# A bias row asked for by another queue, and five pieces of dense work set between score splits, in a two-layer graph and expert kernel

## The chip, the cores and the metric

The kernel runs on one core of a Trainium2 chip. The core has five engines that work side by side, each on its own list of instructions: TensorE (PE in the profile, with its weight loads as PEld), VectorE (DVE), ScalarE (ACT), GpSimd (POOL) and SyncE (SP). SP, ACT and POOL also ask for transfers (DMAs), which 16 DMA engines carry out. The metric is the device time in microseconds (us) of one execution. Before the change the median of 7 runs is 1937.58 us (1932.46 to 1940.60).

## The reference

Two layers work on x, 128 graphs of 64 nodes with 256 features, so 8192 nodes. Each layer has a graph part and a feed-forward part; shortened:

```python
# layer 0, graph part: softplus(xn @ W_self + (I - A_norm) xn @ W_neigh), added to x
# layer 0, feed-forward: every node goes to the one of 8 experts with the highest chance
H = gelu(layernorm(x) @ W1 + b1)                      # 256 -> 1024
probs = softmax(H @ Wg + bg)
assign = argmax(probs)
for e in range(8):
    y = H @ Wd[e] + bd[e]                             # 1024 -> 256; bd[e] is one row of 256
    out = out + where(assign == e, probs[:, e:e+1] * y, 0.0)
x = x + out
# layer 1, graph part: attention inside each graph, layer norm, gelu, added to x
# layer 1, feed-forward: a graph attention over 1048576 edges (and self loops) gives each
# node a score for each of 4 experts
h = (layernorm(x) @ W_gat).reshape(M, HEADS, NUM_EXPERTS)
a_src, a_dst = (h * att_src).sum(-1), (h * att_dst).sum(-1)
e = leaky_relu(a_src[src] + a_dst[dst], 0.2)          # one value an edge and head
alpha = softmax of e over the edges that end in one node
agg = segment_sum(h[src] * alpha, dst)
scores = layernorm(agg).mean over heads
topk_s, topk_i = top_k(scores, 2); w = softmax(topk_s)
for ei in range(4):
    g = where(topk_i == ei, w, 0.0).sum(-1)
    out = out + g * (gelu(z @ W1[ei] + b1[ei]) @ W2[ei] + b2[ei])   # 256 -> 512 -> 256
x = x + out
```

## The kernel before

The nodes are held as 64 tiles of 128 rows, and four tiles (GR) make a group, so there are 16 groups. x stays in on-chip memory for the whole run. The code is a set of Python generators. Each `yield` ends a small piece of work, and the loops that call `next` mix the pieces of several generators. A scheduler then puts the instructions of each engine in an order, from what each depends on, the order in which the code traced them, and a model of their times; inside `with tc.issue_after(i)` an instruction stays behind `i` on its engine. Completion of a transfer that SP or ACT asked for is told by one of eight semaphores. They are handed out in turn, in the scheduler's order, to the transfers of both queues alike. Who takes a semaphore again first waits until the transfer that had it before has landed, whichever queue asked for that one.

**First place: the early slots of layer 0.** A slot is a tile of 128 rows that all belong to one expert. Hidden rows are sent to their expert's place in memory (`hrows`) by POOL, group by group (line 872). Eight slots (EARLY) are already full before the last two groups are through, and `early_slots` (lines 934 to 997) works on them while the last group is finished. It loads two short lists into registers: the rows' places for SP (line 936), the expert numbers for ACT and PE (line 943). For slot t, `load(t)` issues two transposing loads from SP (line 957), three slots ahead (AHEAD); their targets `hT` come from ten buffers (`bh`) that the last group still uses. `bias_of(t)` asks for the expert's bias row, broadcast to 128 partitions (128 KB), into buffer z2 or z3 by turns (lines 969 and 970), from ACT. The first call, `bias_of(0)`, stands ahead of the first loads. Eight matrix products (line 987) make the slot's result, DVE adds the bias row (line 995), and ACT asks for the store of the sum (line 996). So ACT's queue holds in turn: bias 0, bias 1, store 0, bias 2, store 1, bias 3, store 2, and so on. In the same stretch DVE and PE count keys of edges (lines 209 and 348).

**Second place: the scores of the destinations.** After the branch at line 2110 (a rare path for lists that overflow), `td`, 128 x 512 values in f32, is cut into three bf16 pieces `td3`: three copies (line 2322) and two subtractions (line 2324) on DVE. The pieces are later multiplied with one-hot matrices on PE (line 1976), for 16 lists of edges (`edges_of_lists`).

**Units of dense work.** Of layer 1's 16 groups, 8 (DENSE) are put through all four experts before it is known which a node needs. `units = dense()` (lines 1518 to 1537) yields these in units: per group and expert four "h" units (two products, and a gelu on ACT, lines 1490 and 1494) and four "y" units (four products, and DVE's sum with the bias, lines 1500 and 1504). That is 8 x 4 x 8 = 256 units. They are taken as filler all through layer 1, and the trace shows each product of f32 numbers as two: an h unit is four records, a y unit is eight. The takers, in order, are: the end of layer 1's graph part (up to line 1765, filled up to a whole expert); a step after each yield of `prologue` and two `sort`s (lines 2053 to 2055); two in three of the 162 steps of `edges_of_lists` (lines 2349 and 2350); the rest of `sending` (line 2499); a loop that fills up to a whole expert:

```python
            while (n + 1) % (NH1 + GR):
                g, n = next(units)
            adds.append(add)
            for _ in range(1 * (NH1 + GR)):
                g, n = next(units)
```

Up to `adds.append`, each y is stored (line 1527) and read again later (`kept`, line 2371); from there on it is added to x at once (line 2355). What is left of the units runs at the very end, beside `back`:

```python
        steps = back(PARTS - 1)
        for n, _ in enumerate(units):
            next(steps, None)
```

**The pairs and the way back.** The other 8 groups go only to the two experts that a node needs. Their rows are sent to slots, `pairs` runs 38 pairs of slots, and `back(h)` (lines 2466 to 2487) fetches the results for half h: 32 gathers by POOL (line 2474) into seven buffers, and five steps later a copy (line 2480, through 1516) and, for each second one, two weighted sums into x (line 2485) and the store of a finished tile (line 2486). `back(h)` has 37 steps. Its copy is kept behind the last gelu or sum of the unit traced before it (`pace`, line 1515). A gather needs the buffer of the gather seven before, which the copy frees, so gathers go at the pace of the units. `back(1)` is the one that runs at the end, after the last pair.

Of the kernel before, what the change touches and what calls it, by code (L numbers as in the profile page):

```python
# [22 lines left out]
P = 128  # L23
NT = 64
N = P * NT
D = 256
# [61 lines left out]
def kernel(  # L88
# [31 lines left out]
    nc = tc.nc  # L120
# [341 lines left out]
    with tc.tile_pool(name="w0", bufs=1, reuse_waits="tile") as w0, tc.tile_pool(name="kp", bufs=1, reuse_waits="tile") as kp:  # L462
# [30 lines left out]
        with tc.tile_pool(name="bg1", bufs=1, reuse_waits="tile") as bg1, tc.tile_pool(  # L493
# [20 lines left out]
            with tc.tile_pool(name="b2", bufs=1, reuse_waits="tile") as b2, tc.tile_pool(  # L514
# [419 lines left out]
                def early_slots():  # L934

                    _, rows_at = nc.values_load_multi_w_load_instructions(
                        early_row,
                        engines=(mybir.EngineType.SP,),
                        min_val=0,
                        max_val=E0 * N - P,  # L940
                        skip_runtime_bounds_check_because=why,
                    )
                    _, ex = nc.values_load_multi_w_load_instructions(
                        early_e,
                        engines=(mybir.EngineType.Activation, mybir.EngineType.PE),
                        min_val=0,
                        max_val=E0 - 1,
                        skip_runtime_bounds_check_because=why,
                    )
                    loaded = {}  # L950

                    def load(t):

                        loaded[t] = []
                        for i in range(0, FD, GR * P):
                            h = bh.tile([P, GR * P], F32, name="hT")
                            got = nc.sync.dma_start_transpose(
                                h.bitcast(U16).rearrange("p (q r) -> p q r", q=GR),
                                hrows[bass.ds(rows_at[t] * 2, 2 * P), i : i + GR * P],
                            )  # L960
                            for other in sends[-PART * GR :]:
                                tc.declare_no_dep(got.ins, other, reason="rows of an early tile were sent before")
                            loaded[t].append(h)

                    bds_ = {}

                    def bias_of(t):

                        bds_[t] = b2.tile([P, D], F32, name=f"z{2 + t % 2}")
                        nc.scalar.dma_start(bds_[t], f0_bd[bass.ds(ex[t], 1), :].to_broadcast([P, D]))  # L970

                    bias_of(0)
                    for t in range(AHEAD):
                        load(t)
                    yield
                    for t in range(EARLY):
                        if t + AHEAD < EARLY:
                            load(t + AHEAD)
                        if t + 2 == EARLY:
                            y_last = bh.tile([P, GR * P], F32, name="hT")[:, 0:D]  # L980
                        hT = loaded.pop(t)
                        if t + 1 < EARLY:
                            bias_of(t + 1)
                        bd = bds_.pop(t)
                        py = psb.tile([P, GR * P], F32, name="ph")[:, 0:D]
                        for q in range(NH):
                            nc.tensor.matmul(
                                py,
                                hT[q // GR][:, q % GR * P : q % GR * P + P],
                                wd[:, bass.ds(ex[t], 1), q, :].rearrange("p e f -> p (e f)"),  # L990
                                start=(q == 0),
                                stop=(q == NH - 1),
                            )
                        y = y_last if t == EARLY - 1 else b2.tile([P, D], F32, name=f"z{t % 2}")
                        V.tensor_tensor(y, py, bd, ALU.add)
                        nc.scalar.dma_start(yrows[(NSLOT + t) * P : (NSLOT + t + 1) * P, :], y)
                        yield
# [232 lines left out]
                biases = {}  # L1230
                tables, bias = slot_tables(), bias_tables()
                early = early_slots()
                for t, _ in enumerate(early):
                    next(tables, None)
# [283 lines left out]
    def dense():  # L1518

        for g in range(DENSE):  # L1520

            def take(e, k, y):
                if adds:
                    adds[0](GR * g + k, e, y)
                else:
                    n_kept[g] = e + 1
                    behind[:] = [nc.sync.dma_start(ystore[g, k, :, e * D : e * D + D], y).ins]

            if g == 0:
                prepare(0, to)  # L1530
            for n, _ in enumerate(experts(g, take)):

                if n == (0 if to["two"] else NEXP * (NH1 + GR) - GR - 1) and g + 1 < DENSE and g + 1 not in zTs:
                    prepare(g + 1, to)
                yield (g, n)

    units = dense()
# [754 lines left out]
    with tc.tile_pool(name="ga", bufs=1, reuse_waits="tile") as ga, tc.tile_pool(  # L2292
        name="em", bufs=2, reuse_waits="tile"
    ) as emp, tc.tile_pool(name="psm", bufs=1, space=PSUM, reuse_waits="tile") as psm:
        before = ga.tile([P, P], BF16, name="before")
        ones = ga.tile([P, P], BF16, name="ones")


        later = ga.tile([NEXP * RT, NEXP * RT + NEXP], BF16, name="later")
        for v in (before, ones, later):  # L2300
            nc.gpsimd.memset(v, 1.0)
        of_tile = later[:, 0 : NEXP * RT].rearrange("p (e t) -> p e t", e=NEXP)
        of_all = later[:, NEXP * RT :]
        for v, pattern, row, base, op in (
            (before, [[1, P]], -1, 0, ALU.is_gt),
            (of_tile, [[RT, NEXP], [1, RT]], -1, 0, ALU.is_gt),
            (of_tile, [[-RT, NEXP], [0, RT]], 1, 0, ALU.is_ge),
            (of_all, [[-RT, NEXP]], 1, 0, ALU.is_ge),
            (of_all, [[RT, NEXP]], -1, RT, ALU.is_gt),
        ):  # L2310
            nc.gpsimd.affine_select(
                v, v, pattern=pattern, compare_op=op, fill=0.0, base=base, channel_multiplier=row
            )
        iota_s = ga.tile([P, PAIRS], F32, name="iota_s")
        nc.gpsimd.iota(
            iota_s, pattern=[[1, PAIRS]], base=0, channel_multiplier=0, allow_small_or_imprecise_dtypes=True
        )

        td3 = ga.tile([P, 3, NT * 2 * HEADS], BF16, name="td3")
        left_over = td.rearrange("p t c -> p (t c)")  # L2320
        for j in range(3):
            V.tensor_copy(td3[:, j, :], left_over)
            if j < 2:
                V.tensor_tensor(left_over, left_over, td3[:, j, :], ALU.subtract)

        def routes():

            ranks = {}
            for h in range(PARTS):
                yield from gates(ga, T0 + h * RT, T0 + h * RT + RT, ranks)  # L2330
                yield from route(h, ga, ranks, to["ph"])

        steps = routes()
        zeros = ((h, i) for h in range(PARTS) for i in range(PAIRS))
        for taken, _ in enumerate(edges_of_lists(emp, psm, td3)):

            if taken % 3 == 0:
                for h, i in zeros:
                    nc.sync.dma_start(
                        zslots[h][2 * P * i : 2 * P * i + 2 * P].rearrange("(k p) f -> p k f", p=P),  # L2340
                        none.unsqueeze(1).to_broadcast([P, 2, D]),
                    )
                    break
            if taken > ET * (ROUTED // PARTS + 2):
                next(steps, None)

            if taken >= ET * NB:
                next(sending)
            if taken % 3 != 2:
                next(units)  # L2350
        for _ in steps:
            pass
# [229 lines left out]
```

## Time and profile before

| what | value |
|---|---|
| median of 7 runs | 1937.58 us |
| the profiled execution's own time | 1938.42 us |
| its span, first to last instruction | 1936.7 us |
| granted TensorE clock, mean | 0.982 |
| PE busy | 1826.3 us, 94% |
| DVE busy | 1356.6 us, 70% |
| ACT busy | 920.5 us, 48% |
| POOL busy | 444.0 us, 23% |
| early slots' stretch | about 590 to 660 us |
| branch at line 2110, scores, lists | 1297 to about 1560 us |
| pairs | about 1595 to 1874 us |
| last units and the way back | 1874 to 1936.7 us |

The profile is of one execution. Its times count from the first instruction; the time of the run is 1.7 us more than the span. A line of groups or waits names the engine, the tile and the source line. "ACTq" and "SPq" are the queues from which those engines ask for transfers, and "PEldq" is PE's own sequencer. A time in brackets is what the engine stood idle before, with what ended the idle time by the profile's inference.

### The profile page before, as it was taken

The page shows a single profiled execution, that of the slowest core. Times are in us where ns is not written, and L with a number is a line of the kernel's source. Part 1 is how long each engine was busy: PE and PEld are TensorE (multiplying, and loading weights), DVE is VectorE, ACT ScalarE, POOL GpSimd, SP SyncE. Part 2 cuts the span into 40 slices and gives each one's busy share as a digit, 9 for nine tenths or more (in the row PEclk, how much of TensorE's full clock was granted, in tenths as well). Part 3 has the DMA queues.
Part 4 walks back from the last instruction along what each step waited for, and adds up shares of the span by engine and source line. Part 5 has one row for each costly group of instructions (what it writes and reads, how often), then busy time and mean ns, then how long its engine had stood idle before and what let it go on. Part 6 is the DMA issues. An engine that isn't in the chain of part 4 may idle for free. (4 is left out here: it accounts for less than half of the span.)

```text
span 1936.7 us, 31223 instructions
## 1 busy us (share of the span) xinstructions
PE 1826.3 (94%) x10125; PEld 1274.9 (66%) x10125; DVE 1356.6 (70%) x4472; ACT 920.5 (48%) x1612; POOL 444.0 (23%) x465
## 2 busy tenths in 40 slices
PE   7899999998999798899878999999999999999998
PEld 5455555554456687788555666656767768888885
DVE  7798898895668799967598656848888542334435
ACT  4877886886752000000677676323333433334322
POOL 3011111010111011111221000016677633303214
PEclk9999999999999899999979999989999999999999
DMA  9762323242416877698115111562222358979943
GB/s 297 204 194 86 113 71 116 86 141 97 145 74 134 176 172 154 144 180 162 50 60 167 51 55 54 195 184 60 69 53 71 103 166 259 309 241 284 283 140 120
DMA packets 365895, 276.97 MB, mean 143 GB/s; under 512 B 195464, under 2 KB 327456, under 8 KB 365728
## 3 DMA queue, kind: packets, MB, share of 16 engines
q1 hardware_dynamic: 320896, 204.41, 38.3%
q0 software_dynamic: 23040, 60.22, 9.7%
q10 hardware_dynamic: 21792, 10.27, 2.2%
q8 instruction: 86, 1.41, 0.3%
q14 instruction: 81, 0.66, 0.1%
HBM read 115.91 MB, written 123.18 MB: 123 GB/s over the span
## 5 line engine op out<-in xcount | busy, mean ns | idle before, releaser
L505 PE MATMUL ph<-zT,w 128*128 128x512 f32 x512 | 248.4, 610 | 6.1 <-ACT hT L509 6.1
L1348 PE MATMUL py<-wd,hTt 128*128 x960 | 219.5, 382 | 0.0
L1348 PEld LDWEIGHTS py<-wd,hTt 128*128 128x128 f32 x960 | 178.8, 191 | 23.4
L1963 POOL DMA_INDIRECT got<-tsrc,esrc x144 | 155.9, 1083 | 157.0 <-DVE esrc L1934 77.5
L1500 PE MATMUL py<-w,hT 128*128 128x256 f32 x736 | 172.5, 387 | 6.3 <-DVE kt L1902 4.7
L1490 PE MATMUL ph<-zT,w 128*128 128x512 f32 x368 | 169.8, 604 | 0.0
L1356 ACT COPY y<-py 128x256 f32<-128x256 f32 x60 | 22.4, 373 | 290.9 <-PE py L1348 226.5
L1500 PEld LDWEIGHTS py<-w,hT 128*128 128x128 f32 x736 | 138.2, 192 | 32.0 <-issue 8.8
L872 POOL DMA_INDIRECT hrows<-rows,pos x64 | 65.4, 1022 | 395.3 <-ACT wd L654 75.0
L2444 ACT ACTIVATE hT<-ph,b1e 128x256 f32<-128x256 f32 x152 | 72.1, 474 | 172.3 <-PE ph L2440 95.3
L505 PEld LDWEIGHTS ph<-zT,w 128*128 128x128 f32 x512 | 90.6, 193 | 83.5 <-issue 73.1
L1494 ACT ACTIVATE hT<-ph,b 128x512 f32<-128x512 f32 x92 | 63.1, 688 | 165.9 <-PE ph L1490 164.3
L2440 PE MATMUL ph<-zTp,w1e 128*128 128x256 f32 x608 | 137.5, 379 | 0.7 <-ACT zTp L2422 0.7
L2453 PE MATMUL py<-w,hT 128*128 x608 | 137.5, 379 | 0.0
L2461 DVE TENSOR_TENSOR y<-py,b2e 128x256 f32<-128x256 f32 x76 | 32.3, 424 | 149.3 <-PE py L2453 144.7
L668 PE MATMUL pre<-wd 128*128 128x512 f32 x256 | 126.3, 606 | 2.1 <-ACT wd L654 1.3
L509 ACT ACTIVATE hT<-ph,b 128x512 f32<-128x512 f32 x128 | 87.9, 689 | 81.0 <-PE ph L505 77.1
L2440 PEld LDWEIGHTS ph<-zTp,w1e 128*128 128x128 f32 x608 | 115.4, 190 | 16.6 <-ACT zTp L2422 0.9
L808 ACT COPY rows<-tz 128x1024 uint16<-128x1024 uint16 x112 | 110.3, 1020 | 25.8 <-DMA hrows<-rows,pos 13.9
L2453 PEld LDWEIGHTS py<-w,hT 128*128 128x128 f32 x608 | 112.6, 190 | 13.8
L1490 PEld LDWEIGHTS ph<-zT,w 128*128 128x128 f32 x368 | 67.8, 191 | 68.0 <-issue 67.1
L807 PEld LDWEIGHTS tz<-ident,hT 128*128 128x128 f32 x512 | 60.6, 142 | 72.6 <-ACT rows L808 34.3
(505 smaller groups left out, 3748.6 us busy)
## 6 DMA issues: line engine op xcount, KB each, us to landing
w1e<-in_L_ffn_W_dram SPq DMA_DIRECT2D x38, 512.0 KB
yin<-ystore SPq DMA_DIRECT2D x24, 512.0 KB
yrows<-none SPq DMA_DIRECT2D x10, 1024.0 KB
zslots<-none SPq DMA_DIRECT2D x38, 256.0 KB
zin<-zslots SPq DMA_DIRECT2D x38, 256.0 KB
yslots<-y SPq DMA_DIRECT2D x76, 128.0 KB
ystore<-y SPq DMA_DIRECT2D x72, 128.0 KB
x<-in_x_dram SPq DMA_DIRECT2D x8, 1024.0 KB
```

The source lines that it names most:

```text
L505: nc.tensor.matmul(ph, w1[:, c, q * P : q * P + P], zT[:, c, :], start=(c == 0), stop=(c == 1))
L509: gelus.append(S.activation(hT, ph, AF.Gelu, bias=b1[:, q : q + 1]).ins)
L668: nc.tensor.matmul(pre, xnT[:, c, n * P : n * P + P], wcat[:, c, :], start=(c == 0), stop=(c == 1),)
L808: copy(rows[:, :, :, q * P : q * P + P], th.bitcast(U16).rearrange("p (k n h) -> p k h n", k=GR, h=2),)
L872: nc.gpsimd.indirect_dma_start(hrows.rearrange("(r h) f -> r (h f)", h=2), bass.IndirectOffsetOnAxis(ap=pos[:, t : t + 1], axis=0), rows[: ...
L1348: nc.tensor.matmul(py, hT[:, q, :], wd[:, bass.ds(e, 1), q, :].rearrange("p e f -> p (e f)"), start=False, stop=(q == NH - 1),)
L1490: nc.tensor.matmul(ph, w1[:, e, c, q * P : q * P + P], zT[:, c, :], start=(c == 0), stop=(c == 1))
L1500: nc.tensor.matmul(py, hTs[q][:, k * P : k * P + P], w2[:, e, q, :], start=(q == 0), stop=(q == NH1 - 1))
L1963: nc.gpsimd.indirect_dma_start(got, None, tsrc, bass.IndirectOffsetOnAxis(ap=esrc[:, b, at : at + 1], axis=0))
L2440: nc.tensor.matmul(ph, w1e[:, c, q * P : q * P + P], zT[:, c, :], start=(c == 0), stop=(c == 1))
L2444: pace[:] = [S, S.activation(hT, ph, AF.Gelu, bias=b1e[:, q : q + 1]).ins]
L2453: nc.tensor.matmul(py, hTs[q][:, k * P : k * P + P], w2[:, e, q, :].rearrange("p e f -> p (e f)"), start=(q == 0), stop=(q == NH1 - 1),)
```

## The change

There are two edits. In `early_slots`, the expert numbers are loaded into registers of SP too, and the first early slot's bias row (t = 0) is asked for by SP, where it stands ahead of the transposing loads; all later bias rows stay on ACT. In the split of the scores, one unit of dense work is taken from `units` after each copy and after each subtraction, five units in all; nothing is taken out elsewhere.

```diff
                     _, ex = nc.values_load_multi_w_load_instructions(
                         early_e,
-                        engines=(mybir.EngineType.Activation, mybir.EngineType.PE),
+                        engines=(mybir.EngineType.SP, mybir.EngineType.Activation, mybir.EngineType.PE),
                         min_val=0,
                         max_val=E0 - 1,
...
                         bds_[t] = b2.tile([P, D], F32, name=f"z{2 + t % 2}")
-                        nc.scalar.dma_start(bds_[t], f0_bd[bass.ds(ex[t], 1), :].to_broadcast([P, D]))
+                        queue = nc.scalar if t else nc.sync
+                        queue.dma_start(bds_[t], f0_bd[bass.ds(ex[t], 1), :].to_broadcast([P, D]))
...
         for j in range(3):
             V.tensor_copy(td3[:, j, :], left_over)
+            next(units)
             if j < 2:
                 V.tensor_tensor(left_over, left_over, td3[:, j, :], ALU.subtract)
+                next(units)
```

## The prediction

> **What bounds the kernel now.** I read the page first, then the busy times by stretches, then the waits and the timelines at the two places of the change, and last the timeline of the end.
>
> ```profile
> PE 1826.3 (94%) x10125; PEld 1274.9 (66%) x10125; DVE 1356.6 (70%) x4472; ACT 920.5 (48%) x1612; POOL 444.0 (23%) x465
> ```
>
> PE bounds the run as a whole; by stretches (length, then busy time of PE, PEld, DVE, ACT and POOL, the granted clock, the DMA engines' share and GB/s):
>
> ```profile
> 590.00:660.00 70.00, 55.39 (x463) 41.76 (x461) 51.49 (x199) 10.88 (x13) 6.68 (x7) 0.93 0.81 162
> 1256.00:1302.00 46.00, 40.13 (x166) 23.71 (x167) 23.50 (x74) 14.35 (x18) 6.75 (x14) 0.94 0.72 199
> 1302.00:1560.00 258.00, 257.24 (x1759) 182.44 (x1759) 199.17 (x751) 97.43 (x192) 172.46 (x161) 0.99 0.28 75
> ...
> 1596.00:1874.00 278.00, 278.00 (x1363) 244.86 (x1362) 99.24 (x233) 103.84 (x235) 64.20 (x64) 1.00 0.82 260
> 1874.00:1937.00 63.00, 55.21 (x193) 36.24 (x191) 31.77 (x85) 14.51 (x28) 32.16 (x32) 0.98 0.36 111
> ```
>
> From 1302 to 1874 us PE is without a break (257.24 of 258, 278.00 of 278). Whatever is moved about inside that stretch gains nothing. Only the stretches around it have room: 14.6 us idle in the first, 5.9 in the second, 7.8 in the last. The waits of 590 to 680 us show the largest single stall (total, times, longest):
>
> ```profile
> PE pre L348 <- DVE key L209: 13.4, 5, 10.2
> DVE z L995 <- DMA z<-in_L_ffn_bd_dram: 10.7, 1, 10.7
> ```
>
> DVE stands 10.7 us at a slot's sum with its bias row, the key counts behind it on DVE stand too, and PE stands 10.2 us for them. Which row is late, ACT's queue tells (start, duration):
>
> ```profile
> 604.84 0.93 ACTq L970 DMA_DIRECT2D z<-in_L_ffn_bd_dram  x2
> ...
> 614.78 0.34 ACTq L970 DMA_DIRECT2D z<-in_L_ffn_bd_dram  x1
> 625.17 0.35 ACTq L996 DMA_DIRECT2D yrows<-z  x1
> 634.34 0.34 ACTq L970 DMA_DIRECT2D z<-in_L_ffn_bd_dram  x1
> ```
>
> The first two requests, at 604.84, are bias 0 and 1. Bias 2 is asked for at 614.78, bias 3 only at 634.34, and DVE's wait ends at 637.87, at the fourth sum. The late row is bias 3, not bias 0: the first sum ran at 613.75 with no idle time ahead of it. By the trace's semaphore records, store 1 (625.17) waited until the ninth transposing load, issued at 614.85, had landed (625.10), and bias 3 until the tenth, issued at 616.33, had (634.32). Both only take over the semaphore of that load.
>
> At the second place, PE's first work after the branch, and the branch (min/median/max, ns):
>
> ```profile
> 1301.64 1.62 PE L1500 MATMUL py<-w,hT 128*128 128x256 f32 x3 [4.67 <-DVE kt L1902]
> ```
>
> ```profile
> L2110 PEldq COMPARE_BRANCH  x2: 64/2186/4307, 1292.3 to 1297.2; - x2
> ```
>
> The wait is booked on DVE (kt), and the chain of waits runs through the scores there. But PE's own sequencer is in the branch for 4307 ns from 1297.17, which fills 4.31 of the 4.67. No score holds PE.
>
> The end: a gather, PE's last products, the last gather, the copy after the last unit's sum, the last weighted sums.
>
> ```profile
> 1916.37 0.94 POOL L2474 DMA_INDIRECT back<-yslots,place  x1 [0.79 <-DVE yb L1516]
> ...
> 1922.14 7.07 PE L1500 MATMUL py<-w,hT 128*128 128x256 f32 x32
> ...
> 1926.69 0.94 POOL L2474 DMA_INDIRECT back<-yslots,place  x1 [0.70 <-DVE yb L1516]
> ...
> 1929.59 0.28 DVE L1516 COPY yb<-back 128x256 f32<-128x256 f32 x1
> ...
> 1932.78 0.99 DVE L2485 SCALAR_TENSOR_TENSOR x<-yb,weight,x 128x256 f32<-128x256 f32 x2
> ```
>
> PE ends at 1929.21, the run 7.5 us later, since five steps of the way back come after the last unit.
>
> **The change part by part.** *Bias 0 on SP.* SP gains one register load (ACT's took 0.76, SP's own 1.20), a request (0.39 on ACT) and 0.07 to 0.13 of address work: 1.2 to 1.8 us ahead of the first transposing load, which so starts near 597.6 instead of 596.08 and is through SP at 599.1. The second is issued at 600.43 in any case, since it waits 2.78 us for PE to free its buffer. That wait hides SP's added work; without it, up to 1.8 us would pass on to all loads. Nothing else is queued on SP; POOL's queue isn't touched. ACT loses one request of 0.4 us with nothing waiting behind.
>
> What the row itself does: the two rows of 604.84 took 59, 52, 16 and 2% of the DMA engines in the windows of 2 us from 604 to 612, 2.6 us of all sixteen, so 1.3 each. Meanwhile the fifth and sixth transposing loads took 2.71 and 2.36 us of SP against the least of 1.23. From 605 to 640 the DMA engines are at 0.88 to 1.26 of their time; from 596 to 600 at 0.29. So 1.3 us of work leaves the crowded stretch. The tenth load, and with it bias 3, may land 1.3 us earlier; then the eleventh is late next (635.58, before the fifth slot would need it). I take -1.3.
>
> Bounds: if the order of the semaphores shifts so that bias 3 takes another than the tenth load's, PE waits at 634.32 for that load itself, instead of starting the fifth slot at 639.98: -5.6, and -1.8 more if its eight products, 3.76 us after the stall against 1.97 before it, run at full clock. If the cover on SP is gone: +1.8. So -7.4 to +1.8. I stay near the small end because the turn of the semaphores stays the same: bias 0 and the loads only change places at the head of the row, and store 1 and bias 3 come as many transfers later as before.
>
> A rule that speaks against this part: the Trainium skill, "DMA: Bandwidth & Descriptors", section "Issuing engines are not separate DMA queues", has all queues end on the same 16 engines, so that another issuer saves issue time alone. By it alone this part gains at most ACT's 0.4 us, and the sum would be +7.6 instead of +6.7.
>
> *Five units among the scores.* The five DVE operations (three of 0.42, two of 0.68 us) remain. PE gets five units (a unit is 6.87/4 = 1.72 us) ahead of the lists. Nothing there waits for DVE, so the move by itself is worth 0; what hides it is PE's unbroken work to 1874. Bounds: -4.7, if units closed all of the wait; +1.5, the two waits of 0.69 and 0.86 us that PE has now at 1559 and 1562, if they came twice. I take 0, by the branch's row.
>
> But units are counted, and the fill loop rounds up. Stored results:
>
> ```profile
> L1527 SPq DMA_DIRECT2D ystore<-y x72: 319/320/667, 1278.1 to 1584.2; - x72
> L1527 SPq DMA_DIRECT2D ystore<-yin x36: 319/320/527, 1053.6 to 1256.3; - x36
> ```
>
> 108 stored y are 27 experts, 216 units. They come about as 72 (the graph part, 36 stores) + 20 (prologue 8 yields, two sorts 6 each) + 108 (two in three of 162) + 14 (32 yields of `sending` less 18) = 214, and 2 to fill the expert. With five more it is 219, and the loop takes 5 to fill 224. Then eight units with direct sums, as now. So 24 units are left for the end instead of 32: one expert, 8 x 1.72 = 13.8 us of PE, moves from behind the pairs to ahead of them. PE's sum stays, and it ends at 1929.2 as before. Four results more are stored and read again, 1.0 MB, which PE's work hides.
>
> The way back doesn't move with it. It can only start when the last pair is stored, now 13.8 us later (first gather 1877.08, then 1890.9), and 37 steps have 24 units beside them, not 32. After the last unit 13 steps remain instead of 5. Gather 25 (counting from 0) needs the buffer that the copy after the last unit frees: 1916.37 + 13.77 = 1930.14. The six after it follow at POOL's free rate, 1.25 us (1877.08, 1878.33, 1879.58): the last at 1937.64. A gather lands 2.7 to 3.3 us after its issue (least, median): 1940.3 to 1940.9. Copy and two sums take 1.2 (1932.57 to 1933.77), store and close 2.9 (1933.77 to 1936.7): 1944.4 to 1945.0, so +7.7 to +8.3. I take +8.0. DVE isn't late: 13 steps at 0.6 are done at 1938. If the copies ran ahead of the last unit, the cost would fall towards 0; `pace` keeps them behind it. If each gather took the 1.48 of the slowest free step, +9.4.
>
> Sum: -1.3 + 0 + 8.0 = +6.7. The profiled execution, 1938.42 with a span of 1936.7, would be 1945.1; it lies 0.84 above the median of the runs, so I forecast 1937.58 + 6.7 = 1944.3.
>
> **The rivals.** *The stall goes (not slower).* The added register load and request shift the loads in the scheduler's order past store 0 and bias 2; bias 3 inherits a semaphore long free and is issued with store 1 or before. Price -5.6 to -7.4, so +0.6 to +2.4 in all: 1938.2 to 1940.0. For it: in the order of the requests the loads stand close around store 0. Against: store 1 itself needed from 625.17 to 635.41 to land in the same crowd, and bias 3 would follow behind it. It decides from 4.1 us of gain on, where the whole comes under 0.2%.
>
> *The branch's wait is DVE's (not slower).* If the profile's booking is right, five units close 4.7 us: 1944.3 - 4.7 = 1939.6. The branch's 4307 ns speaks against it. A page would speak for it: the Trainium skill, "Advanced Engine Details and Errata", section "Control Flow Timing", gives a compare-and-branch about 108 ns; by it 4.2 us would be left to DVE and the sum would be +2.5; PE's row has forty times that figure.
>
> *The end isn't longer.* If the units' count comes to the same multiple of eight, or the gathers run ahead of the units, only -1.3 is left: 1936.3. Against it stand the count and the seven buffers.
>
> *SP's cover is gone.* The loads come 1.8 later and the stall with them, no gain: +9.8, 1947.4.
>
> **How the numbers follow.** 0.2% (3.9 us) is about what a measurement of this kernel can tell from no change. Forecast, slower: 0.64; cover gone, slower: 0.12; the stall goes: 0.12, of which 0.02 on to faster; DVE's wait closed: 0.04, same; end not longer: 0.08, of which 0.03 faster. Same holds 0.10 + 0.04 + 0.05 = 0.19; faster 0.05; slower 0.76. The range reaches from the case in which the stall goes (1938.2) to the lost cover (1947.4), with half a microsecond at each end for the median's own spread. The likeliest case alone has 1942 to 1946.
>
> **What would show it.** Right: the stored y's after the graph part grow from 72 to 76, 24 units after the last pair, about 8 us more between PE's last product and the end; the fourth sum's wait for its bias still near 9 us. Wrong: no wait at that sum; PE's first product after the branch without its gap; gathers that all come before PE's end.

## The result and the profile after

The changed kernel takes 1945.38 us in the median of 19 runs (1939.75 to 1950.39), the kernel before 1937.58 in 46. The ratio is 1.0042, with a 95% interval from 1.0033 to 1.0051. That is 8.1 us slower (6.4 to 9.9); the prediction had 6.7 us.

One profiled execution misleads here. That of the changed kernel took 1940.16 us, 5.2 less than its median, and its span is 1938.4 us against 1936.7 before. Read by the two spans alone, the change would cost 1.7 us. What that execution had, and a second profiled execution of the same kernel hadn't, is found below.

The page's line for PE, and the stretches of the changed kernel (length, busy time of PE, PEld, DVE, ACT and POOL, granted clock, DMA share, GB/s):

```profile
PE 1831.0 (94%) x10125; PEld 1278.0 (66%) x10125; DVE 1359.9 (70%) x4474; ACT 921.7 (48%) x1612; POOL 443.8 (23%) x465
```

```profile
590.00:660.00 70.00, 64.74 (x502) 48.14 (x501) 60.09 (x245) 12.24 (x15) 8.04 (x8) 0.93 0.82 180
1256.00:1302.00 46.00, 42.20 (x168) 26.89 (x168) 21.74 (x67) 13.66 (x17) 6.74 (x14) 0.96 0.67 180
1302.00:1560.00 258.00, 256.45 (x1762) 181.31 (x1761) 196.28 (x736) 100.53 (x195) 175.43 (x160) 1.00 0.28 73
1596.00:1874.00 278.00, 277.33 (x1360) 244.11 (x1359) 102.05 (x240) 102.62 (x233) 64.08 (x64) 1.00 0.82 261
1874.00:1938.00 64.00, 47.12 (x171) 32.11 (x169) 31.45 (x85) 12.31 (x24) 31.90 (x32) 0.90 0.38 115
```

PE still has no break worth naming from 1302 to 1874 us (256.45 of 258, 277.33 of 278). The two ends of the table have moved in opposite directions. In the early slots PE is busy for 64.74 us of 70, where it was 55.39. In the last stretch it is busy for 47.12 of 64, where it was 55.21 of 63.

The waits of 590 to 680 us, SP's first requests and its tenth transposing load, ACT's queue and POOL's first send of the last group, all of this execution:

```profile
PE pre L348 <- DVE key L209: 4.3, 5, 2.1
...
DVE z L996 <- DMA z<-in_L_ffn_bd_dram: 1.1, 1, 1.1
```

```profile
599.67 1.36 SPq L957 DMA_TRANSPOSE hT<-hrows  x1
601.89 0.39 SPq L971 DMA_DIRECT2D z<-in_L_ffn_bd_dram  x1
...
618.37 1.23 SPq L957 DMA_TRANSPOSE hT<-hrows  x1
```

```profile
608.36 0.39 ACTq L971 DMA_DIRECT2D z<-in_L_ffn_bd_dram  x1
...
619.26 0.36 ACTq L997 DMA_DIRECT2D yrows<-z  x1
619.84 0.50 ACTq L971 DMA_DIRECT2D z<-in_L_ffn_bd_dram  x1
623.18 0.35 ACTq L997 DMA_DIRECT2D yrows<-z  x1
623.75 0.37 ACTq L971 DMA_DIRECT2D z<-in_L_ffn_bd_dram  x1
```

```profile
620.07 1.14 POOL L872 DMA_INDIRECT hrows<-rows,pos  x1 [23.25 <-issue]
```

The fourth sum waited 1.1 us for its bias row instead of 10.7. Bias 0, which the source has ahead of the transposing loads, goes out behind the first of them: the scheduler has put it there, at 601.89. The lines of ACT's queue are, in order, bias 1, store 0, bias 2, store 1 and bias 3. Bias 3 went out at 623.75, 3.7 us after POOL's first send; before it went out at 634.34, 19.3 us after that send (615.01). It still takes over the semaphore of the tenth transposing load. But that load was issued at 618.37, 1.7 us ahead of the first send, and by its semaphore's records had landed at 621.69; bias 3 came right behind store 1, which stands ahead of it in ACT's queue. Before, the load was issued at 616.33, 1.3 us behind the first send, and needed until 634.32.

The branch and PE's first work after it:

```profile
L2111 PEldq COMPARE_BRANCH  x2: 64/1726/3389, 1286.3 to 1291.2; - x2
```

```profile
1294.77 2.47 PE L1501 MATMUL py<-w,hT 128*128 128x256 f32 x5 [3.75 <-DVE td L2326]
```

PE's gap of 4.67 us has become one of 3.75. The branch in it has gone from 4307 to 3389 ns, and the gap has shrunk by no more than that. The five units haven't closed it.

The stored results, and the end: PE's last products, copies and gathers of the way back, the last weighted sums; then, before and after, the closing instruction on POOL's queue (its longest record is the one at the end).

```profile
L1528 SPq DMA_DIRECT2D ystore<-y x76: 319/320/1502, 1271.9 to 1588.0; - x76
```

```profile
1914.05 7.07 PE L1501 MATMUL py<-w,hT 128*128 128x256 f32 x32
...
1921.49 0.28 DVE L1517 COPY yb<-back 128x256 f32<-128x256 f32 x1
...
1922.05 0.94 POOL L2477 DMA_INDIRECT back<-yslots,place  x1 [0.78 <-DVE yb L1517]
...
1928.59 0.95 POOL L2477 DMA_INDIRECT back<-yslots,place  x1 [0.30 <-DVE x L2488]
...
1929.84 0.95 POOL L2477 DMA_INDIRECT back<-yslots,place  x1 [0.30 <-DVE x L2488]
...
1932.68 0.29 DVE L1517 COPY yb<-back 128x256 f32<-128x256 f32 x1 [0.54 <-DMA back<-yslots,place]
1932.89 1.00 DVE L2488 SCALAR_TENSOR_TENSOR x<-yb,weight,x 128x256 f32<-128x256 f32 x2
```

```profile
L2577 POOLq DRAIN  x3: 40/112/7946, 1926.5 to 1936.4; - x3
```

```profile
L2580 POOLq DRAIN  x3: 40/113/11766, 1925.8 to 1938.1; - x3
```

76 results are stored after the graph part instead of 72, so 24 units are left behind the last pair. PE ends at 1921.12, and seven gathers are issued after that, the last at 1929.84. The last sums end at 1933.89 and the run at 1938.4, so PE's last product is 17.3 us ahead of the end, against 7.5 before. The close itself has changed hands. POOL's DRAIN ends at 1937.56, and the run 0.86 us after it; SP, which waits for the last store, was through at 1936.19. Before, the DRAIN ended at 1934.41, and SP was the last with 1935.83.

### The profile page after: what moved, and what is told of

The parts are those of the page before. It is cut to its first block, busy times and chain, and to the rows that moved or that the text cites. A ratio compares the mean times of both kernels' runs of the same rounds, so it can differ in the third digit from the quotient of the medians.

```text
span 1938.4 us, 31245 instructions
## 1 busy us (share of the span) xinstructions
PE 1831.0 (94%) x10125; PEld 1278.0 (66%) x10125; DVE 1359.9 (70%) x4474; ACT 921.7 (48%) x1612; POOL 443.8 (23%) x465
```

## The experiments

The twelve runs were made in four sets, each on one chip, and each ratio is to runs of the kernel before on the same chip. The chips differ: the kernel before took 1959.4, 1965.2 and 1958.4 us (medians) on those of the first three sets, and 1939.9 on that of the last. So only ratios are compared between sets. A difference in microseconds is the ratio times the median of before, with the interval's ends in brackets.

### First set: each edit alone, and the tail

The first edit alone:

```diff
-                        engines=(mybir.EngineType.Activation, mybir.EngineType.PE),
+                        engines=(mybir.EngineType.SP, mybir.EngineType.Activation, mybir.EngineType.PE),
...
-                        nc.scalar.dma_start(bds_[t], f0_bd[bass.ds(ex[t], 1), :].to_broadcast([P, D]))
+                        queue = nc.scalar if t else nc.sync
+                        queue.dma_start(bds_[t], f0_bd[bass.ds(ex[t], 1), :].to_broadcast([P, D]))
```

> Only the first edit: bias 0 is asked for by SyncE. Theory A (a race decides the early slots, the tail sets the rest): the wait of the fourth sum for its bias row is short where the loads get ahead of the last group's sends and about 10 us where they don't; if the tail alone costs 9.8 us, as the two profiles have it (17.3 us from PE's last product to the end against 7.5), then 8.1 - 9.8 = -1.7 us is left for this edit as a median: 1935.9 us, with PE's end to the run's end still 7.5 us. Theory B (the stall is gone for good, as the one profile of the changed kernel shows it): -9 us, 1928.6, and the second edit costs 17. Theory C (as predicted): -1.3 us, 1936.3, the fourth sum's wait still near 9 us.

Measured: 0.9982 [0.9959, 1.0004], -3.5 us (-8.0 to +0.8). PE's gap at the fourth sum was 3.1 us.

The second edit alone:

```diff
             V.tensor_copy(td3[:, j, :], left_over)
+            next(units)
             if j < 2:
                 V.tensor_tensor(left_over, left_over, td3[:, j, :], ALU.subtract)
+                next(units)
```

> Only the second edit: five units among the score splits. Theory A: +9.8 us less the 0.9 by which PE's gap after the branch was shorter, 1946.5 us, 24 units after the last pair, about 17 us from PE's last product to the end, the fourth early sum's wait near 10 us again in most executions. Theory B: +17 us, 1954.6. Theory C (as predicted): +8.0 us, 1945.6.

Measured: 1.0079 [1.0050, 1.0109], +15.5 us (9.8 to 21.4); 17.3 us from PE's last product to the end; PE's gap at the fourth sum 10.5 us.

The tail alone:

```diff
-            for _ in range(1 * (NH1 + GR)):
+            for _ in range(2 * (NH1 + GR)):
```

> The kernel before with eight units more taken by the loop after adds.append: nothing among the score splits, bias 0 on ACT, but 24 units left for the end as in the changed kernel. If the second edit costs only by the units that the end loses: the same as with the second edit alone, +8 to +10 us (1945.6 to 1947.6), about 17 us from PE's last product to the end. If it is the place among the scores that costs: within 2 us of the kernel before, 1935.6 to 1939.6.

Measured: 1.0045 [1.0016, 1.0074], +8.8 us (3.1 to 14.5); 17.3 us from PE's last product to the end. The last stores and the last gather of the way back of this kernel:

```profile
1954.10 10.78 SPq L2486 DMA_DIRECT2D out_dram<-x  x7
...
1960.42 0.95 POOL L2474 DMA_INDIRECT back<-yslots,place  x1 [0.30 <-DVE x L2485]
```

PE's last product ends at 1951.69, 8.7 us ahead of that gather. The loss of eight units at the end costs this by itself, with nothing put among the scores. The second edit cost 6.7 us more than that, with intervals that overlap, so its place came into question.

The tail the other way:

```diff
-            for _ in range(1 * (NH1 + GR)):
+            for _ in range(0 * (NH1 + GR)):
```

> The kernel before with eight units fewer taken there, so 40 are left for the end. Theory of the tail: all 37 steps of the way back have a unit beside them, PE's last product comes when it did, and the end is set by the last unit's sum and its store, 3 to 4 us after PE instead of 7.5: -3.7 us, 1933.9 us. Rival: the pairs can't start 13.8 us earlier, because their rows or weights aren't there, and PE stands before them: 0 to +13.8 us.

Measured: 1.0012 [0.9988, 1.0035], +2.4 us (-2.4 to +6.9). The end came 3.9 us after PE's last product, as the tail theory has it. PE's timeline ahead of the first pair shows that the rival came true as well:

```profile
1597.83 2.11 PE L1500 MATMUL py<-w,hT 128*128 128x256 f32 x9
1604.89 1.11 PE L2420 MATMUL ph<-ident,zin 128*128 128x128 f32 x4 [4.96 <-DMA zin<-zslots]
```

PE stands 4.96 us for the rows of the first pair (`zin`). What the end gained was lost there.

### Second set: the whole change once more, and the place of the five units

The whole change:

> The changed kernel unaltered, for a second profile and a ratio beside the next three. Three parts are now in question: early slots (-7 in the run with the first edit alone, where PE's gap at the fourth sum was 3.1 us instead of 7.8 to 10.5), tail (+9.9, 17.3 us from PE's last product to the end instead of 7.4), and the place of the five units, which may cost about 7 us (1976.5 with the second edit against 1969.4 with the tail alone). Theory D (place costs): +8 to +10 us over the kernel before, and PE stands at waits for gathered rows between 1302 and 1600 us longer than in the kernel before. Theory A (place is free): +1 to +3 us.

Measured: 1.0075 [1.0054, 1.0095], +14.7 us (10.6 to 18.7); 17.3 us from PE's last product to the end. The early slots of this execution, waits and ACT's queue:

```profile
PE pre L348 <- DVE key L209: 13.6, 5, 10.1
DVE z L996 <- DMA z<-in_L_ffn_bd_dram: 10.6, 1, 10.6
```

```profile
622.71 0.35 ACTq L997 DMA_DIRECT2D yrows<-z  x1
631.00 0.34 ACTq L971 DMA_DIRECT2D z<-in_L_ffn_bd_dram  x1
```

The wait is back at 10.6 us, with bias 0 on SP: store 1 goes out at 622.71, and bias 3 not before 631.00. The tenth load was issued 0.18 us after the first send. So the edit doesn't take the stall away for good; the table over all profiles, below, shows how often it came.

The first edit alone, again:

> Only the first edit, once more beside the others of this set. Both theories: -3 to -9 us; the fourth sum's wait for its bias row at most 4 us, since the tenth transposing load is issued at most about 0.3 us after the last group's first send, where it was 1.3 to 1.7 us after it with bias 0 on ACT.

Measured: 0.9986 [0.9966, 1.0007], -2.8 us (-6.7 to +1.4), gap 2.3 us.

The second edit with the count kept:

```diff
             V.tensor_copy(td3[:, j, :], left_over)
+            next(units)
             if j < 2:
                 V.tensor_tensor(left_over, left_over, td3[:, j, :], ALU.subtract)
+                next(units)
...
-                g, n = next(units)
+                if taken < 11:
+                    g, n = next(units)
```

> The second edit with the count kept: five units among the score splits, three fewer beside the sends of rows after the lists, and the fill loop then takes none, so 32 units are left for the end as before; bias 0 on ACT. Theory A (PE bounds the lists, units may be moved about in front of the pairs at no cost): within 1.5 us of the kernel before. Theory D (the lists are set by POOL's gathers, and what PE does ahead of them delays these): +5 to +8 us, the last gather of source rows 6 to 8 us later than in the kernel before, PE's last product to the end still 7.4 us.

Measured: 1.0044 [1.0024, 1.0064], +8.6 us (4.7 to 12.6), with 7.5 us from PE's last product to the end. So on this chip the place costs about as much as the tail. The busy times from 1305 to 1560 us, of this kernel, of the first edit alone on the same chip, and of the kernel before, show what is different here:

```profile
1305.00:1560.00 255.00, 238.70 (x1613) 166.14 (x1614) 177.35 (x673) 83.92 (x165) 143.60 (x135) 0.96 0.24 57
```

```profile
1305.00:1560.00 255.00, 239.15 (x1655) 168.77 (x1654) 177.69 (x684) 84.90 (x170) 148.26 (x143) 0.96 0.24 57
```

```profile
1305.00:1560.00 255.00, 254.24 (x1752) 180.07 (x1752) 199.17 (x751) 97.43 (x192) 172.46 (x161) 1.00 0.28 75
```

In the execution that the prediction was made from, PE was busy for 254.24 of 255 us. On this chip it is busy for 239, with the five units or without. What it waits for (this kernel, total, times, longest):

```profile
PEld ps L2008 <- DVE r L1880: 13.1, 6, 3.5
...
PE ps L2008 <- DVE r L1880: 9.8, 6, 2.6
...
PE ps L1913 <- DVE acc L2013: 3.2, 2, 2.6
```

PE and its weight loads stand for DVE's results of the lists (`r`, `acc`), and DVE at other times for PE. PE no longer sets the pace alone, so units put ahead of the lists can delay them: PE's first product after the branch is followed 24.1 us later by the tenth gather of source rows, against 16.2 with the first edit alone. The chain then takes as long as ever (235.7 and 236.8 us from the tenth gather to the last). But from the last gather to the first pair it is 66.3 us against 71.4, so from PE's first product to the first pair the two profiles differ by 1.7 us only. Of the 6.8 us between their spans, 5.7 lie ahead of that product, where bias 0 is on ACT in the one and on SP in the other. That the place costs 8.6 us is measured; that the delayed lists are the way in which it costs this isn't shown. What makes the chain longer than the 208.6 us of the prediction's execution wasn't found: POOL's median time for a gather is the same (945 and 946 ns).

Bias 0 on SP with 36 units left for the end:

```diff
-            for _ in range(1 * (NH1 + GR)):
+            for _ in range(NH1):
```

> The first edit, and four units fewer ahead of the pairs, so 36 are left for the end beside 37 steps of the way back. With 40 left the end was 3.8 us after PE's last product but PE stood 5.0 us before the first pair; with 36 the pairs would start 6.9 us earlier, not 13.8, and that gap should be 0. Tail theory: the end comes 4 to 5 us after PE instead of 7.4, so -3, and -3 to -7 by the early slots: -6 to -10 us. Rival (the pairs can't start earlier, or the end doesn't shorten): no better than the first edit alone.

Measured: 0.9982 [0.9962, 1.0001], -3.5 us (-7.5 to +0.2), less than expected. The end came 5.1 us after PE and PE stood 1.0 us at the fourth sum, but the pairs and the end now held 4.0 us of PE's idle time that they hadn't held.

### Third set: two corrections that didn't help

Two bias rows on SP:

```diff
-                        engines=(mybir.EngineType.Activation, mybir.EngineType.PE),
+                        engines=(mybir.EngineType.SP, mybir.EngineType.Activation, mybir.EngineType.PE),
...
-                        nc.scalar.dma_start(bds_[t], f0_bd[bass.ds(ex[t], 1), :].to_broadcast([P, D]))
+                        queue = nc.scalar if t > 1 else nc.sync
+                        queue.dma_start(bds_[t], f0_bd[bass.ds(ex[t], 1), :].to_broadcast([P, D]))
                     bias_of(0)
+                    bias_of(1)
...
-                        if t + 1 < EARLY:
+                        if 1 < t + 1 < EARLY:
```

> The first edit carried one row further: bias 0 and bias 1 both asked for by SyncE ahead of the transposing loads, so no bias row lands among loads 4 to 6; nothing else. Race theory: no load before the last group's sends holds SyncE longer than 1.7 us (now one holds it 2.5 to 4.3 us), the tenth load is issued at least 2 us ahead of the first of these sends, PE's gap at the fourth sum is under 1.5 us instead of 7.6 to 10.5, in each execution: -7 to -10 us. Rival (the rows cost SyncE as much ahead of the loads as they cost beside them, and the tenth load meets the sends as before): PE's gap stays at 2 to 10 us, 0 to -3 us.

Measured: 0.9999 [0.9982, 1.0016], nothing. The order of requests came out as meant, though by less than the 2 us expected: the tenth load was issued 1.0 us ahead of the first send, and bias 3 went out early (ACT's queue, then DVE's fourth sum):

```profile
621.09 0.38 ACTq L971 DMA_DIRECT2D z<-in_L_ffn_bd_dram  x1
```

```profile
636.30 0.42 DVE L997 TENSOR_TENSOR z<-ph,z 128x256 f32<-128x256 f32 x1 [5.25 <-DMA z<-in_L_ffn_bd_dram]
```

But the row asked for at 621.09 held the sum up until 636.30, for 5.25 us of idle time. With the wait for the semaphore gone, the row's own way through the crowded DMA engines is what comes last. In the changed kernel's first execution a row asked for as early (3.7 us after the first send) was used 9.5 us after its request. Why it wasn't here is open.

Eight units taken from ahead of the branch and put ahead of the pairs:

```diff
+        early = [8]
         for of in (prologue(to["tz"], pp), sort(lists[0], pp, psm), sort(lists[1], pp, psm)):
             for _ in of:
-                next(units)
+                early[0] -= 1
+                if early[0] < 0:
+                    next(units)
...
-            for _ in range(1 * (NH1 + GR)):
+            for _ in range(2 * (NH1 + GR)):
```

> The place turned round: eight units fewer ahead of the branch (those beside the prologue), eight more just ahead of the pairs, 32 left for the end as before; bias 0 on ACT. Theory D (on these chips the lists are set by POOL's gathers, and PE waits for them between 1302 and 1560 us): PE's gap after the branch ends up to 13.8 us earlier, and what of that the prologue's other work allows is gained: -4 to -12 us. Theory A (PE bounds this part): 0, within 2 us, or slower by what PE stands in the prologue.

Measured: 1.0026 [1.0007, 1.0045], +5.1 us (1.4 to 8.8), the wrong sign. In its profile the branch comes at 1281.9 and the last gather of source rows at 1531.5, 14 and 19 us earlier than in the kernel with two rows on SP on the same chip (1295.6 and 1550.1). But this execution was the fastest of the kernel's twelve (1957.98 against a median of 1963.47), so its profile doesn't show where the others lose. That starting the lists sooner helps as much as starting them later hurts is refuted; the reason is open.

All of it together (the last two edits, and `NH1 + GR + NH1` in the last line):

> Both of these, and 36 units left for the end: two bias rows on SyncE, eight units fewer ahead of the branch. The sum of the parts: -7 to -10 by the early slots, -3 by the end, -4 to -12 by the lists under theory D or 0 under A: -14 to -25 us under D, -10 to -13 under A.

Measured: 1.0021 [1.0004, 1.0038], +4.1 us (0.8 to 7.4). The parts don't add up, since two of them weren't gains.

### Fourth set: the changed kernel with its end given back

```diff
-            for _ in range(1 * (NH1 + GR)):
+            for _ in range(0 * (NH1 + GR)):
```

> The changed kernel with its end given back: the eight units after adds.append aren't taken there, so 32 are left for the end as in the kernel before. The end: 7.4 us from PE's last product instead of 17.3. Without the tail's 9.8 us two parts are left, the early slots and the place of the five units. If the place costs what it did with the count kept (+8.6 us): +5 to +7 us over the kernel before, and PE's time from its first product after the branch to the first pair some 6 us longer than in the kernel before (the fill adds a whole expert, but it drops the eight units after it, so the count ahead of the pairs is 224 as before). If the place is free: -1 to -3 us.

Measured: 0.9980 [0.9965, 0.9995], -3.9 us (-6.8 to -1.0): 1935.66 against 1939.94 us, faster than the kernel before. (It wasn't run beside the changed kernel.) The end came 7.7 us after PE. This chip is like that of the first result, and there the place of the five units costs nothing that can be seen: PE is busy for 254.55 of the 255 us from 1305 to 1560.

```profile
1305.00:1560.00 255.00, 254.55 (x1750) 180.52 (x1750) 190.87 (x710) 96.92 (x191) 166.54 (x153) 0.99 0.28 69
```

The tenth gather also comes late here, 22.2 us after PE's first product behind the branch instead of 15.5. But from the last gather to the first pair it is 62.2 us, where it was 69.4, and the whole way from that product to the first pair is as long as before (293.4 and 293.5 us). PE sets the pace, and what is put ahead isn't left over behind. The early slots of this execution had the full stall:

```profile
PE pre L348 <- DVE key L209: 13.7, 5, 10.6
DVE z L996 <- DMA z<-in_L_ffn_bd_dram: 11.1, 1, 11.1
```

It took 1940.58 us, the second slowest of its twelve; the fastest three took 1931.2 to 1931.6. The 9 us between them are about the size of the stall, which fits that the stall is in the one and not in the others; only the one was profiled.

### The early slots, over all profiles

Times from POOL's first send of the last group to three events, and PE's gap at the fourth sum, in us, from the records of each profiled execution:

| kernel | 10th load issued | bias 3 asked for | fourth sum | PE's gap |
|---|---|---|---|---|
| before | +1.3 | +19.3 | +22.9 | 10.2 |
| second edit alone | +1.6 | +20.5 | +24.6 | 10.5 |
| tail 24 | +0.6 | +16.3 | +21.5 | 7.8 |
| tail 40 | +1.6 | +18.6 | +23.1 | 9.0 |
| five units, count kept | +1.1 | +16.4 | +22.6 | 7.6 |
| lists sooner | +1.1 | +14.0 | +20.6 | 5.7 |
| whole change, first profile | -1.7 | +3.7 | +13.2 | 0.6 |
| whole change, second profile | +0.2 | +13.4 | +25.3 | 10.1 |
| first edit alone | +0.3 | +11.6 | +19.0 | 3.1 |
| first edit alone, again | -0.1 | +8.8 | +18.2 | 2.3 |
| first edit, 36 left | -0.4 | +8.6 | +16.0 | 1.0 |
| whole change, end given back | +0.2 | +14.1 | +23.2 | 10.6 |
| two rows on SP | -1.0 | +3.7 | +18.9 | 4.7 |
| all together | -2.5 | +3.8 | +20.7 | 4.7 |

With bias 0 on ACT (the first six) the tenth load is issued 1.2 us behind the first send on average; with it alone on SP (the next six) 0.3 us ahead of it. That is 1.5 us of shift, and it is enough to bring the two to about the same moment. Where the load is issued ahead of the first send, bias 3 is asked for 3.7 to 8.8 us after that send; where it is issued behind it, 11.6 to 20.5 us. It isn't one step between two sides: in the twelve profiles whose semaphore records show it, issue times spread over 3.3 us go with landings from 1.6 to 20.5 us after the send, mostly the later the later the load was issued.

The request isn't the whole of the stall, though. In all fourteen profiles the fourth sum starts 0.12 us after bias 3 has landed. In the first six kernels the row needs 3.4 to 6.5 us from request to landing, in the other eight, where it is asked for earlier, 7.3 to 16.8. So a part of what the earlier request gains is lost again on the row's way, and two kernels with bias 0 on SP (the second profile of the whole change, and the one with its end given back) still have the full stall.

## Why the prediction was right, and where it was wrong

**The end** (+8.0 taken). Right in sign, cause and nearly in size: 9.8 us in the two profiles (17.3 against 7.5), and 17.3 us in all four profiles with 24 units left, 3.9 with 40. Of the prediction's terms, the gathers after PE's end took 8.72 us (8.43 foretold), landing and copy 2.84 (2.7 to 3.3), copy and sums 1.21 (1.2). The mis-sized term is "store and close 2.9": it took 4.5 us, and 4.5 to 4.6 in the other three kernels with 24 left, against 2.9 to 3.1 with 32, 36 and 40. The traces show what the sum left out. In all fourteen profiles POOL's DRAIN ends 6.8 us after the end of POOL's last gather, and the run can't close before that. With 32 units or more the DRAIN is over before SP has seen the last store land; with 24 the last gather is so late that the DRAIN comes last, 1.4 us after SP in the changed kernel. Without these 1.4 us the end would have cost 8.4 us by estimate, close to the 8.0 taken.

**The bias row** (-1.3 taken). The size is about right as a median: -3.5 and -2.8 alone, both intervals with 0 in them, -3.9 (-6.8 to -1.0) with the units' place in it, and 8.1 - 9.8 = -1.7 by difference. The mechanism was right in one half: bias 3 keeps the semaphore of the tenth load, and the load moves ahead by 1.5 us. The step that failed is "the tenth load, and with it bias 3, may land 1.3 us earlier". The landing doesn't follow the issue one to one: the same 1.5 us bring the load to about the moment of the sends, where it may land early or late, the row itself takes 3.4 to 16.8 us, and PE's gap is then between 0.6 and 10.6 us. That -1.3 came near the median's gain is luck. So "the fourth sum's wait near 9 us" was wrong for the first profile (1.1) and right for two others (10.6 and 11.1). The rival in which the stall goes had the right place, but for another reason than it gave: no shift of the semaphores, and only in some executions. The rival "SP's cover is gone" didn't come true: bias 0 went out behind the first load, not ahead of all loads as the prediction has it, and the wait ahead of the second load shrank from 2.78 to 1.40 us and hid it.

The Trainium skill, "DMA: Bandwidth & Descriptors", section "Issuing engines are not separate DMA queues", has another issuer save issue time alone. The profiles show that an order in time comes with it: bias 0 is asked for 2.2 us after the first load instead of 8.8, and the tenth load moves by 1.5 us against the sends. Whether the median gains more by this than ACT's 0.4 us, only the last run shows, with the units' place in it.

**The five units' place** (0 taken, -4.7 to +1.5). Right on the first chip and on that of the last set, as far as their profiles show PE without a break. On the chip of the second set it cost 8.6 us (4.7 to 12.6), outside the bounds. "What hides it is PE's unbroken work to 1874" was read from one execution, and there it holds; where the lists' chain is 229 to 238 us long instead of 209, PE has 16 us of gaps, and the cover that the prediction counted on isn't there. By which way the move then costs 8.6 us stays open. On that chip the parts add up: -2.8 + 8.6 + 9.8 = 15.6, and the whole change cost 14.7.

**The branch.** Right: the wait booked on DVE was the branch's. It stayed at 3.7 to 5.3 us in every profile, and the branch itself at 3.3 to 4.8 us, with the five units behind it or not. The 108 ns that the prediction takes from the Trainium skill, "Advanced Engine Details and Errata", section "Control Flow Timing", lie among PE's other compare-and-branches (64, 98 and 313 ns in the kernel before), far from this one.

**The count.** Right: 224 units ahead of the pairs without direct sums and eight with them, 24 left, 76 stored results. The rivals "the end isn't longer" and "DVE's wait" fell with it.

So the forecast of 1944.3 us came near the measured 1945.38 for the reason that it gave as the main one, the tail. The 1.4 us that are missing are less than what either of the smaller parts is uncertain by.

## What to carry to other kernels

Where filler work is handed out by count and rounded up to whole blocks, an edit that takes a few pieces early is paid for at the other end: count the pieces, and ask what ran beside those that the end has lost. What a transfer gains that is moved ahead near the start of a crowd isn't the shift of its issue: here issue times within 3.3 us went with landings from 1.6 to 20.5 us after the crowd's first send, so the cost is spread over the executions, and one profile shows one of its ends. Here the run closed only when POOL was through with its last gathers: a path that ends behind the last store isn't seen when only the store is followed. "PE is busy throughout, so moving work about is free" holds only for the chip and the execution that were looked at; where another chain is nearly as long, the place can count as well.

## What was not expected

- The kernel before took 1937.6 and 1939.9 us (medians) in the first result and the last set, and 1958 to 1965 us on the chips of the other three sets. Most of the difference lies between the branch and the first pair, where PE is idle for 13 to 22 us in the profiles of the first three sets, and for 2.2 to 2.5 in the others.
- A bias row of 128 KB asked for 3.7 us after the sends began was used 9.5 us after its request in one execution and 15.2 in another, with DVE waiting for it in both.
- POOL's DRAIN at the end of the run takes until 6.8 us after its last gather, in every profile. The close after the last store's sums took 2.9 to 3.1 us where that was hidden, and 4.5 to 4.6 with 24 units left.
